# Second layer of a graph network: products with a window of B, from two row groups of the array back into one

## The chip, the cores and the metric

The kernel runs on one core of a Trainium2 chip. Its time is the device time of one execution in microseconds (us); before the change the median of 5 runs is 3966.8 us (3966.45 to 3967.49).

The core has five engines with queues of their own: PE (TensorE, matrix products; its weight loads are listed as PEld), DVE (VectorE, element by element), ACT (ScalarE, activations), POOL (GpSimd, here above all gathers by index) and SP (SyncE, which issues DMA transfers). An engine runs its own instructions in order, and semaphores make one engine wait for another.

## The reference, cut to what matters

There are 12500 nodes with 64 features, and 212500 edges sorted by their target `dst` (12500 of them are loops from a node to itself). Two layers follow each other, each behind a layer norm and a relu:

```python
# layer 1: one 64x64 weight for each of 16 types of edges
msg = sum over r of (h[src] * (etype == r)) @ weight[r]
x = x + segment_sum(msg, dst)

# layer 2: a two-layer network on each edge
hid = relu(concat(h[src], h[dst], edge_attr_8) @ W1 + b1)
x = x + segment_sum(hid @ W2 + b2, dst)
```

W1 has 64 + 64 + 8 rows. So `concat(...) @ W1 + b1` is A[src] + B[dst] + attr @ W1c, with A = h @ W1a + b1 and B = h @ W1b, one row for each node, and W1c the last 8 rows of W1.

## The kernel before, in words

Edges are handled in tiles of P = 128, and G = 4 tiles make a group. Without the loops there are 1563 tiles in 391 groups (the last group has 3). Since edges are sorted by target, the targets of a group lie within a window of W = 40 consecutive nodes, whose first row is read from a table at run time.

The first layer gathers rows of h for each tile and adds them into a table by target and type with one-hot products. As blocks of two times 128 nodes are completed, it makes the rows of A (`a_rows`, for the first four groups `a_early`) and of B (`b_rows`) and stores them. Beside it, in pieces, it sorts the edges' words: `dst_l` gets the place of each edge's target in its group's window, `turned_c` the attributes of the edges (8 rows of 128 edges for a tile), `attr_l` those of the loops.

`second_layer` (line 1449) does the rest, in 391 iterations and some more for the lags. For iteration `it`, with g = it:

- `gather` (line 1005) issues four gathers on POOL, each of 128 rows of A by the tile's sources, into one of 14 buffers of the pool `land` (line 316).
- SP loads the window of B's rows (40 rows of 64) into `b_win[g % 6]`. Below it, `b_win` holds the 8 rows of W1c, loaded once.
- PE makes `pz`, the part of the edges' hidden layer that doesn't come from A: for each tile one product of K = 48 rows. The weights (`of_edges`, 48x128) are the one-hot of the target's place (40 rows) and the edge's attributes (8 rows), and `b_win` moves through.
- Line 1532, three iterations later: DVE adds the gathered rows, `z = pz + a`. Line 1541, four later: ACT makes `hid` = relu(z), and DVE a one-hot `oh` of the place for each edge. Line 1554, six later: PE sums hid over the edges of each target (`pa`). Line 1566, nine later: DVE adds `pa` into `sums`. Towards the end of the run these lags shrink to one or two iterations (`turns`, line 129).
- The one-hot in `of_edges` is made by ACT in two passes, from the places that SP has loaded, the same on all 40 rows (`local_bc`): `off` = |place - row|, then relu(1 - off). The negative row numbers are `neg_w`.

Each product is done in float32, which the trace shows as two MATMUL records, each with its weight load.

Before the change, even and odd tiles of a group use different rows of the array: even tiles have their one-hot, attributes and B rows at partitions 0 to 47, odd tiles at 64 to 111. So B's rows are loaded twice for each group (into both halves), `dst_l` is stored in two rows (even and odd tiles), and `pz` lies in two banks, one for each half. `load_edges` loads places and attributes for a block of RB = 4 groups, a block ahead; `one_hots` makes one half of a block in one call (two passes of 40x1024), in every second iteration, for the block after the present one.

Besides, every eight groups two blocks of 128 nodes become complete: `results` (line 1422) multiplies `sums` with W2, adds x and has ACT issue the store `out<-o`; `own_edges` (line 1400) does the loops of two blocks.

The order is the program's: `V_, S_, T_, Q_, P_` (line 348) issue each instruction behind the one issued last on the same engine, so that DVE, ACT, PE, SP and POOL take the second layer in the order in which the loop body names its instructions. Nearly every one of them is recorded under line 340, the helper that issues them, so the tiles' names tell them apart in the profile.

Of the kernel before, what the change touches and what calls it, by code (L numbers as in the profile page):

```python
# [42 lines left out]
F32 = mybir.dt.float32  # L43
BF16 = mybir.dt.bfloat16
I32 = mybir.dt.int32
AF = mybir.ActivationFunctionType
ALU = mybir.AluOpType
# [5 lines left out]
P = 128  # L53
N = 12500
D = 64
R = 16
EA = 8
# [3 lines left out]
NB = -(-N // P)  # L61
# [12 lines left out]
G = 4  # L74
W = 40
# [9 lines left out]
NGC = -(-NTC // G)  # L85
# [26 lines left out]
KLN = 60  # L112
# [66 lines left out]
WE = W + EA  # L179
EARLY = 4  # L180
NBW = 6
RG = 8
RB = 4
# [26 lines left out]
def gnn_kernel(  # L210
# [13 lines left out]
    attr_c = dram.tile([EC * EA, 1], F32, name="attr_c")  # L224
    attr_l = dram.tile([NB * P * EL, 1], F32, name="attr_l")
    turned_c = dram.tile([NGC * G * EA, P], F32, name="turned_c")
    turned_l = dram.tile([NB * EL, P], F32, name="turned_l")
    src_e = dram.tile([EARLY * 2, 2 * P], I32, name="src_e")
    dst_l = dram.tile([2, NGC * G // 2 * P], BF16, name="dst_l")
    edges_c = dram.tile([EC * 2, 1], I32, name="edges_c")  # L230
# [19 lines left out]

    neg_w = keep.tile([P, 1], F32, name="neg_w")
    for h in range(2):
        G_.iota(neg_w[h * D :][:D], pattern=[[0, 1]], base=0, channel_multiplier=-1, allow_small_or_imprecise_dtypes=True)

# [58 lines left out]
    def in_order():  # L313
        with ExitStack() as c2:
# [98 lines left out]

            b_win = [own.tile([P, D], F32, name=f"b_win{k}") for k in range(NBW)]
            NHID = 6
# [12 lines left out]
            def weights():  # L428
                for k in range(2):
                    Q_.dma_start(wrel[k * D : (k + 1) * D], w_rel[k::2].rearrange("r i o -> i r o"))  # L430
                    Q_.dma_start(w1ab[k * D : (k + 1) * D], w1[: 2 * D].rearrange("(k i) o -> i k o", k=2))
                    yield
                Q_.dma_start(b1_bc, b1.unsqueeze(0).to_broadcast([P, D]))
                Q_.dma_start(t_loop[N:, :].rearrange("n o -> o n"), none)
                Q_.dma_start(attr_l[N * EL :, :].rearrange("(n c) o -> n (c o)", c=EL), zero[: NB * P - N, :EL])
                for t in hid_l:
                    V_.memset(t[:, :, D:], 1.0)
                yield
                Q_.dma_start(w1c, w1[2 * D :])
                Q_.dma_start(place_row, step_2.unsqueeze(0))  # L440
                yield
                Q_.dma_start(w2b[:D, :], w2)
                Q_.dma_start(w2b[D:DA, :], b2.unsqueeze(0))
                yield
                Q_.dma_start(b_rows[NB * P :, :], zero[:W])
                for b in (NB - 2, NB - 1):
                    Q_.dma_start(a_early[b * P : (b + 1) * P, :], zero)
                yield
# [5 lines left out]
            def weights_of_attributes():  # L454
                for t in b_win:
                    for h in range(2):
                        Q_.dma_start(t[h * D + W : h * D + WE, :], w1[2 * D :])
                    yield
# [13 lines left out]
            def places_of(c, psA):  # L472
# [16 lines left out]
                V_.tensor_copy(o[:n], d[:n])  # L489
                for i in range(2):  # L490
                    Q_.dma_start(dst_l[i, b0 // 2 * P : (b0 // 2 + n) * P].rearrange("(r e) -> r e", e=P), o[:n, i, :])
                if c == 0:
# [108 lines left out]
            def loop_attrs(q, psA):  # L601
# [12 lines left out]
                shape, shape2 = [P, m, SUB], [P, m, IN_SUB]  # L614
                V_.tensor_single_scalar(to, firsts, float(NB * P - KLN), op=ALU.min)
                V_.tensor_scalar(to, to, 0.0, float(EL), op0=ALU.max, op1=ALU.mult)
# [832 lines left out]
            def second_layer(ps):  # L1449
# [10 lines left out]
                at, at_b = {}, {}  # L1460
                edges, loaded_edges = {}, {}
                EB = RB * G * P // 2

                def load_edges(b):
                    n = min(EB, NGC * G // 2 * P - b * EB)
                    if n <= 0:
                        return
                    place = wk2.tile([P, EB], BF16, name="local_bc", bufs=2)
                    e = wk2.tile([P, EB], F32, name="of_edges", bufs=3)
                    words = turned_c[b * 2 * EB // P * EA : (b * EB + n) * 2 // P * EA, :].rearrange("(t h c) e -> h c t e", h=2, c=EA)  # L1470
                    for h in range(2):
                        Q_.dma_start(
                            place[h * D : h * D + W, :n], dst_l[h : h + 1, b * EB : b * EB + n].to_broadcast([W, n])
                        )
                        Q_.dma_start(e[h * D + W : h * D + WE, :n].rearrange("c (t e) -> c t e", e=P), words[h])
                    loaded_edges[b] = place, e, n

                def one_hots(b, h):
                    if b not in loaded_edges:
                        return  # L1480
                    place, e, n = loaded_edges[b]
                    rows = slice(h * D, h * D + W)
                    off = wk2.tile([P, EB], BF16, name="off")
                    S_.activation(off[rows, :n], place[rows, :n], AF.Abs, bias=neg_w[rows])
                    S_.activation(e[rows, :n], off[rows, :n], AF.Relu, bias=1.0, scale=-1.0)
                    edges[b] = e

                load_edges(0)
                for h in range(2):
                    one_hots(0, h)  # L1490
                of_z, of_hid, of_pe, of_add = (turns(lag, NGC) for lag in (L2_Z, L2_HID, L2_PE, L2_ADD))
                for it in range(NGC + L2_ADD[1]):

                    g = it
                    if g < NGC:
                        if g % RG == 0:
                            at_b.update(enumerate(windows(first_row, g, PAD_DST, Q_, min(RG, NGC - g)), g))
                        if g % RB == 0:
                            load_edges(g // RB + 1)
                        a_of[g], n_of[g] = gather((a_early if g < EARLY else a_rows)[:, :], src_c, g, NTC)  # L1500
                        n = n_of[g]
                        if n:
                            bw = b_win[g % NBW]
                            now = bass.ds(at_b.pop(g), W)
                            for h in range(2):
                                Q_.dma_start(bw[h * D : h * D + W, :], b_rows[now, :])
                            if g == 1:
# [3 lines left out]
                                for _ in sources_of_last(range(2, EARLY), wk2):  # L1511
                                    pass
                            if g % RB == 0:
                                pz = ps.tile([P, 2, RB, G // 2, D], F32, name="pz", bufs=2)
                            pz_of[g] = pz[:, :, g % RB].rearrange("p h j d -> p j h d")
                            for i in range(n):
                                j, h = divmod(i, 2)
                                at_e = slice((g % RB * G // 2 + j) * P, (g % RB * G // 2 + j + 1) * P)
                                rows = slice(h * D, h * D + WE)
                                more = range(2 if g < EARLY else 0)  # L1520
                                T_.matmul(
                                    pz_of[g][:, j, h, :], lhsT=edges[g // RB][rows, at_e], rhs=bw[rows], start=True, stop=not more
                                )
                                for b in more:
                                    T_.matmul(
                                        pz_of[g][:, j, h, :],
                                        lhsT=of_last[g][b][:, i * P : (i + 1) * P],
                                        rhs=a_last[:, b, :],
                                        start=False,
                                        stop=(b == 1),  # L1530
                                    )
                    for g in of_z.get(it, []):
                        n = n_of[g]
                        if n:
                            hid_of[g] = wk2.tile([P, G, D], F32, name="z", bufs=3)
                            z, a = (t.rearrange("p (j h) d -> p j h d", h=2) for t in (hid_of[g], a_of.pop(g)))
                            pz_g = pz_of.pop(g)
                            for j, h in ((slice(0, n // 2), slice(0, 2)), (slice(n // 2, n // 2 + 1), slice(0, n % 2))):
                                if n % 2 or h.stop == 2:
                                    V_.tensor_tensor(*(t[:, j, h, :] for t in (z, pz_g, a)), op=ALU.add)  # L1540
                    for g in of_hid.get(it, []):
# [12 lines left out]
                    for g in of_pe.get(it, []):  # L1554
                        n = n_of[g]
                        if n:
# [4 lines left out]
                            for i in range(n):  # L1561
                                T_.matmul(pa_of[g], lhsT=r[:, i, :], rhs=o[:, i, :], start=(i == 0), stop=(i == n - 1))
                    if it % 2:
                        one_hots(it // RB + 1, it % RB // 2)
                    next(open_step, None)
# [510 lines left out]
```

## Time and profile before

| | before |
|---|---|
| median of 5 runs | 3966.8 us |
| the profiled execution | 3965.02 us |
| its span, first to last instruction | 3963.1 us |
| first gather of the second layer | 1999.9 us |
| last gather issued | 3952.27 us |
| gathers of the second layer | 1547 of a_rows, 16 of a_early |
| records of pz<-b_win,of_edges on PE | 3126, mean 433 ns |
| loads b_win<-b_rows | 782, 10 KB each |
| loads local_bc<-dst_l | 194 of 80 KB, 2 of 60 KB |
| mean granted clock of TensorE | 0.530 |

The profile comes from one execution, whose span of 3963.1 us lies 1.9 us below its own time. Times of single instructions are from it. Each group of instructions is named by what it writes and reads: `pz<-b_win,of_edges` are the products with the window of B. "Idle before" is the time that the engine had nothing to do just ahead of such instructions, with what ended it. Matmuls are pipelined, so the mean duration of one is longer than the time from one to the next. Gathers overlap in another way: what POOL is busy with is the issuing of a gather, and the rows land later.

### The profile page before, as it was taken

The numbers are of one execution on the slowest core, as the hardware profiler recorded it, in microseconds if no ns is written. First come the engines' busy times: TensorE is split into PE (matmuls) and PEld (weight loads), VectorE is DVE, ScalarE is ACT, GpSimd is POOL, SyncE is SP. The second block draws the span as 40 slices with busy tenths as digits, with TensorE's granted clock in tenths as the row PEclk, the third lists the DMA queues.
The fourth block names the chain that finished last, engine by engine and source line by source line (L and its number), as shares of the span: only waits on it lengthen the run. The fifth ranks groups of instructions, "written<-read, shape, count | busy, mean of one in ns | idle before, by whom it ended". The sixth has DMA issues, their size and how long they took to land. (4 is left out here: it accounts for less than half of the span.)

```text
span 3963.1 us, 53034 instructions
## 1 busy us (share of the span) xinstructions
PE 2186.3 (55%) x14955; PEld 1601.4 (40%) x14955; DVE 1418.8 (36%) x4924; ACT 1647.0 (42%) x3341; POOL 2984.7 (75%) x3170
## 2 busy tenths in 40 slices
PE   1545555555665666666685555555555555555544
PEld 0433333333333333333364444444444444444444
DVE  7895764744743333333321111111111111111112
ACT  6654545544554555554533333323233333333322
POOL 7777777777777777777777777777777777777776
PEclk9655555555555555555555555555555555555555
DMA  5424324225335333333232222222222222222221
GB/s 136 97 46 88 74 46 86 48 46 120 59 49 93 59 59 56 53 57 55 48 66 48 51 48 51 48 51 48 51 48 50 49 48 52 47 52 47 52 47 38
DMA packets 569509, 234.60 MB, mean 59 GB/s; under 512 B 455824, under 2 KB 497680, under 8 KB 568950
## 3 DMA queue, kind: packets, MB, share of 16 engines
q0 software_dynamic: 101152, 111.42, 15.7%
q1 hardware_dynamic: 454757, 116.50, 14.0%
q10 hardware_dynamic: 13298, 3.20, 0.4%
q8 instruction: 123, 2.02, 0.2%
q14 instruction: 179, 1.47, 0.1%
HBM read 195.55 MB, written 35.25 MB: 58 GB/s over the span
## 5 line engine op out<-in xcount | busy, mean ns | idle before, releaser
L340 POOL DMA_INDIRECT rows<-a_rows,src_c x1547 | 1462.1, 945 | 471.6 <-issue 398.5
L340 POOL DMA_INDIRECT rows<-h_rows,src_c x1533 | 1455.0, 949 | 473.3 <-issue 395.9
L340 PE MATMUL pa<-oh_r,rows 128*64 128x96 f32 x6132 | 810.3, 377 | 763.6 <-DMA rows<-h_rows,src_c 614.4
L340 PEld LDWEIGHTS pa<-oh_r,rows 128*64 128x64 f32 x6132 | 470.5, 203 | 1140.3 <-DMA rows<-h_rows,src_c 703.9
L340 DVE TENSOR_TENSOR z<-pz,rows 128x256 f32<-128x256 f32 x392 | 166.0, 423 | 1519.2 <-DMA rows<-a_rows,src_c 1474.5
L340 ACT ACTIVATE hid<-z 128x256 f32<-128x256 f32 x391 | 161.8, 414 | 1075.5 <-DVE z L340 1010.3
L340 DVE TENSOR_TENSOR table<-table,pa 128x96 f32 x1565 | 393.5, 251 | 521.2 <-PE pa L340 439.1
L340 PE MATMUL pa<-oh,hid 128*65 128x40 f32 x3126 | 426.4, 311 | 277.0 <-DVE sums L340 222.7
L340 ACT ACTIVATE off_r<-iota_s,code 128x192 bf16<-128x192 f32 x1535 | 569.7, 444 | 0.0
L340 PE MATMUL pz<-b_win,of_edges 48*128 48x64 f32 x3126 | 504.7, 433 | 79.9 <-ACT of_edges L340 45.0
L340 PEld LDWEIGHTS pa<-oh,hid 128*65 128x65 f32 x3126 | 372.4, 226 | 329.9 <-issue 228.2
L340 PEld LDWEIGHTS pz<-b_win,of_edges 48*128 48x128 f32 x3126 | 412.8, 318 | 144.6 <-ACT of_edges L340 61.8
L340 ACT ACTIVATE oh_r<-off_r 128x768 f32<-128x768 bf16 x392 | 330.2, 842 | 94.5 <-PE pa L340 83.8
L340 ACT ACTIVATE off<-local_bc,neg_w 40x1024 bf16<-40x1024 bf16 x196 | 222.5, 1135 | 5.6 <-DMA local_bc<-dst_l 2.9
L340 ACT ACTIVATE of_edges<-off 40x1024 f32<-40x1024 bf16 x196 | 206.2, 1052 | 6.3
L340 PE MATMUL pT<-table,wrel 128*64 128x256 f32 (+1 forms) x800 | 201.7, 601 | 0.0
L340 DVE SCALAR_TENSOR_TENSOR table<-b_rel,rsel,hT 128x256 f32<-128x256 f32 (+1 forms) x400 | 168.7, 467 | 88.5 <-PE hT L340 67.3
L340 DVE COPY_PREDICATED k_a<-move,k_a 128x1712 int32<-128x1712 int32 (+8 forms) x124 | 186.1, 1501 | 2.1 <-issue 0.2
L340 PE MATMUL po<-ident,hid_l 128*65 128x128 f32 x196 | 54.5, 432 | 200.0 <-ACT hid_l L340 200.0
L340 PE MATMUL po<-w1c,o_at 8*128 8x64 f32 x196 | 53.2, 423 | 170.7 <-DVE sums L340 170.7
L340 PE MATMUL po<-w2b,sums 65*128 65x64 f32 x196 | 53.6, 428 | 156.1 <-DVE sums L340 156.1
L340 ACT COPY table<-table 128x1024 f32<-128x1024 f32 x49 | 51.2, 1044 | 186.3 <-DVE table L340 186.3
(242 smaller groups left out, 1540.7 us busy)
## 6 DMA issues: line engine op xcount, KB each, us to landing
rows<-a_rows,src_c POOLq DMA_INDIRECT x1547
rows<-h_rows,src_c POOLq DMA_INDIRECT x1533
local_bc<-dst_l SPq DMA_DIRECT2D x194, 80.0 KB
b_win<-b_rows SPq DMA_DIRECT2D x782, 10.0 KB
k_a<-in_attr_k SPq DMA_DIRECT2D x72, 144.0 KB
k_a<-in_attr SPq DMA_DIRECT2D x52, 132.0 KB
u_in<-attr_c SPq DMA_DIRECT2D x97, 64.0 KB
turned_c<-u_out SPq DMA_DIRECT2D x97, 64.0 KB
```

The costliest lines, as they stand in the source:

```text
L340: last_ins[self.engine] = getattr(self.engine, name)(*args, **kw)
```

## The change

- The one-hots, attributes and B's rows go back to partitions 0 to 47 for all tiles. `b_win` is 48 rows high, `neg_w` 40.
- B's rows are loaded once for each group, and the attribute weights once for each buffer.
- `dst_l` is stored as one row for each group, in one store where there were two.
- Places and attributes are loaded in one transfer each for a block of four groups, in the block's first iteration, into three buffers each; they were loaded in two transfers each, a block ahead, into two and three buffers.
- The one-hots are made for two groups at a time (again two passes of 40x1024), at the head of every second iteration, just ahead of the products that read them.
- `pz` is a bank for two groups, four buffers of it; z is one addition for the last group too, where it was two.
- `attr_l` gets room for KLN = 60 more nodes, and the clamp of a scatter's first place moves accordingly. This has to do with the first layer only.

The order of the instructions on PE and of the gathers on POOL is the same in both kernels, and so is that on DVE, but for the last group's z. SP has 1959 instructions instead of 2937.

The diff, cut to its core:

```diff
-    dst_l = dram.tile([2, NGC * G // 2 * P], BF16, name="dst_l")
+    dst_l = dram.tile([NGC, G * P], BF16, name="dst_l")
...
-            b_win = [own.tile([P, D], F32, name=f"b_win{k}") for k in range(NBW)]
+            b_win = [own.tile([WE, D], F32, name=f"b_win{k}") for k in range(NBW)]
...
-                Q_.dma_start(attr_l[N * EL :, :].rearrange("(n c) o -> n (c o)", c=EL), zero[: NB * P - N, :EL])
+                Q_.dma_start(attr_l[N * EL :, :].rearrange("(n c) o -> n (c o)", c=EL), zero[: NB * P + KLN - N, :EL])
...
-                    for h in range(2):
-                        Q_.dma_start(t[h * D + W : h * D + WE, :], w1[2 * D :])
+                    Q_.dma_start(t[W:, :], w1[2 * D :])
...
-                for i in range(2):
-                    Q_.dma_start(dst_l[i, b0 // 2 * P : (b0 // 2 + n) * P].rearrange("(r e) -> r e", e=P), o[:n, i, :])
+                Q_.dma_start(dst_l[b0 // G : (b0 + nt) // G, :].rearrange("g (h e) -> (g h) e", h=2), o[:n].rearrange("r i e -> r (i e)"))
...
-                def load_edges(b):
...
-                def one_hots(b, h):
...
-                load_edges(0)
-                for h in range(2):
-                    one_hots(0, h)
...
                         if g % RB == 0:
-                            load_edges(g // RB + 1)
+                            ng = min(RB, NGC - g)
+                            local_bc = wk2.tile([W, RB * G * P], BF16, name="local_bc", bufs=3)
+                            Q_.dma_start(
+                                local_bc[:, : ng * G * P],
+                                dst_l[g : g + ng, :].rearrange("g e -> (g e)").unsqueeze(0).to_broadcast([W, ng * G * P]),
+                            )
+                            of_edges = wk2.tile([WE, RB * G * P], F32, name="of_edges", bufs=3)
+                            Q_.dma_start(
+                                of_edges[W:, : ng * G * P].rearrange("c (t e) -> c t e", e=P),
+                                turned_c[g * G * EA : (g + ng) * G * EA, :].rearrange("(t c) e -> c t e", c=EA),
+                            )
...
-                            now = bass.ds(at_b.pop(g), W)
-                            for h in range(2):
-                                Q_.dma_start(bw[h * D : h * D + W, :], b_rows[now, :])
+                            Q_.dma_start(bw[:W, :], b_rows[bass.ds(at_b.pop(g), W), :])
...
-                            if g % RB == 0:
-                                pz = ps.tile([P, 2, RB, G // 2, D], F32, name="pz", bufs=2)
-                            pz_of[g] = pz[:, :, g % RB].rearrange("p h j d -> p j h d")
+                            if g % 2 == 0:
+                                np_ = min(2, NGC - g)
+                                cols = slice(g % RB * G * P, (g % RB + np_) * G * P)
+                                off = wk2.tile([W, 2 * G * P], BF16, name="off")[:, : np_ * G * P]
+                                S_.activation(off, local_bc[:, cols], AF.Abs, bias=neg_w)
+                                S_.activation(of_edges[:W, cols], off, AF.Relu, bias=1.0, scale=-1.0)
+                                pz = ps.tile([P, 2, G, D], F32, name="pz", bufs=4)
+                            pz_of[g] = pz[:, g % 2]
                             for i in range(n):
-                                j, h = divmod(i, 2)
-                                at_e = slice((g % RB * G // 2 + j) * P, (g % RB * G // 2 + j + 1) * P)
-                                rows = slice(h * D, h * D + WE)
+                                k = (g % RB * G + i) * P
                                 more = range(2 if g < EARLY else 0)
-                                T_.matmul(
-                                    pz_of[g][:, j, h, :], lhsT=edges[g // RB][rows, at_e], rhs=bw[rows], start=True, stop=not more
-                                )
+                                T_.matmul(pz_of[g][:, i, :], lhsT=of_edges[:, k : k + P], rhs=bw, start=True, stop=not more)
...
-                            z, a = (t.rearrange("p (j h) d -> p j h d", h=2) for t in (hid_of[g], a_of.pop(g)))
-                            pz_g = pz_of.pop(g)
-                            for j, h in ((slice(0, n // 2), slice(0, 2)), (slice(n // 2, n // 2 + 1), slice(0, n % 2))):
-                                if n % 2 or h.stop == 2:
-                                    V_.tensor_tensor(*(t[:, j, h, :] for t in (z, pz_g, a)), op=ALU.add)
+                            V_.tensor_tensor(hid_of[g][:, :n, :], pz_of.pop(g)[:, :n, :], a_of.pop(g)[:, :n, :], op=ALU.add)
...
-                    if it % 2:
-                        one_hots(it // RB + 1, it % RB // 2)
```

## The prediction

> **What bounds the kernel now.** I read the busy shares first, then the costliest groups, the waits of POOL, and a stretch of the second layer, where every edited instruction but a few stands.
>
> ```profile
> PE 2186.3 (55%) x14955; PEld 1601.4 (40%) x14955; DVE 1418.8 (36%) x4924; ACT 1647.0 (42%) x3341; POOL 2984.7 (75%) x3170
> ...
> L340 POOL DMA_INDIRECT rows<-a_rows,src_c x1547 | 1462.1, 945 | 471.6 <-issue 398.5
> L340 POOL DMA_INDIRECT rows<-h_rows,src_c x1533 | 1455.0, 949 | 473.3 <-issue 395.9
> ...
> L340 DVE TENSOR_TENSOR z<-pz,rows 128x256 f32<-128x256 f32 x392 | 166.0, 423 | 1519.2 <-DMA rows<-a_rows,src_c 1474.5
> ```
>
> POOL is busy for only 75%, but nearly all of the rest is the gap ahead of each gather: 471.6 us / 1547 = 0.305 us, put down to "issue", a wait for nothing that the profile shows. The waits of POOL say whether a gather is ever held for longer than that (columns: total us, times, longest us):
>
> ```profile
> POOL rows L340 <- issue: 799.0, 2621, 0.3
> POOL rows L340 <- DMA rows<-a_rows,src_c: 71.6, 235, 0.3
> POOL rows L340 <- DMA rows<-h_rows,src_c: 60.1, 197, 0.3
> ...
> POOL rows L340 <- DVE odds L340: 3.5, 1, 3.5
> POOL rows L340 <- DMA attr_c<-k_a,k_to: 3.0, 3, 1.6
> POOL attr_c L340 <- DMA u_in<-attr_c: 2.6, 1, 2.6
> ```
>
> The first three have a longest of 0.3 us, the same gap under other names. So a gather takes 0.945 + 0.30 = 1.25 us whatever the others do, and the real waits of POOL in the whole span are 3.5 + 3.0 + 2.6 us and a 1.1 us one, all in the first layer. The second layer has 1563 gathers (1547 and 16 of a_early): 1563 x 1.249 = 1952 us, from 1999.9 to 3953.2. The group of z above says the same from the other side: 1474.5 of DVE's 1519.2 us of idle time ahead of z are waits for gathered rows, not for the products pz. The page's chain of waits reaches back only 13 us from the end and cannot show this.
>
> Then one stretch of the steady second layer (columns after the stretch: busy us and count of PE, PEld, DVE, ACT, POOL; granted clock, DMA share, GB/s), beside the busiest stretch that DVE has in the first layer:
>
> ```profile
> 200.00:300.00 100.00, 47.76 (x453) 37.12 (x449) 89.81 (x237) 57.34 (x134) 75.73 (x80) 0.60 0.24 49
> ...
> 3000.00:3100.00 100.00, 52.94 (x348) 46.23 (x348) 18.63 (x72) 30.17 (x42) 75.58 (x80) 0.50 0.23 48
> ```
>
> Both hold 80 gathers, with DVE at 90% and at 19%. PE, DVE and ACT have 47, 81 and 70 us of every 100 us left in the second layer. **The kernel ends when the last gather has ended, plus a tail of 10 us.** An edit counts only if it touches POOL's gathers, holds one of them up, or lies in that tail.
>
> **The change, part by part.**
>
> *POOL.* Its order of gathers is unchanged; one of two iotas for neg_w goes (0.32 us for two, so 0.16 us) ahead of the first gather at 3.3 us. At 50.6 us POOL waits 3.5 us for DVE (odds, the row above), which hides it: 0. If that cover were gone: -0.2 us.
>
> *PE, the products with B.* The count stays: 4 matmuls a group, two records each, in the same order among the others. What goes is that they alternate between rows 0 to 47 and 64 to 111 of the array. The time of it is in the timeline of PE (start, us, operation, records):
>
> ```profile
> 2019.18 1.11 PE L340 MATMUL pz<-a_last,raw_rows 128*128 128x64 f32 x4
> 2020.23 0.69 PE L340 MATMUL pz<-b_win,of_edges 48*128 48x64 f32 x2
> ...
> 3006.84 1.12 PE L340 MATMUL pz<-b_win,of_edges 48*128 48x64 f32 x8
> 3007.89 1.10 PE L340 MATMUL pa<-oh,hid 128*65 128x40 f32 x8
> ```
>
> From start to next start, 8 records in two row groups take 1.05 us, and 4 records of the same shape that use all rows also take 1.05 us (2019.18 to 2020.23). po<-w1c, with 8 rows only, takes 1.04 us for 4 (2025.21 to 2026.25), so it isn't the number of rows. I take 2.10 us for a group in place of 1.05: +1.05 us. Between 2100 and 3900 us are 1441 gathers, 360 groups, and PE is busy for 959 us; 959 + 360 x 1.05 = 1337 us, 74% of 1800. Cover: 1.29 us of idle PE a group stay. Cost 0. From the other side, if the records overlapped as now, 0 too; if each waited out its own 433 ns (mean of the group), it is the first rival.
>
> The Trainium skill, "TensorE: Matmul & The Clock Gate", decision table, speaks against this change: products over few rows, laid on separate row groups, run concurrently, and one alone takes as long as one over 128 rows. By that rule, on a path that PE sets, 391 x 1.05 = 411 us would come on top; the rows above agree on the factor of 2, but they put it on an engine that waits.
>
> *ACT, the one-hots.* 196 pairs of 40x1024 before; 391 groups by two make 196 pairs after, the same elements: 1135 + 1052 ns each, 0 difference in busy time. They move: before they are made a block of four groups ahead, after in the iteration that needs them, ahead of hid of group g-4. This adds a wait: off of group g waits on ACT for the load of the same block. Behind it on ACT stand hid, hid_l and the store of the output, and pa on PE and the sums on DVE wait for hid. A pz(g) is needed only when the gathers of g have landed. In PE's order it follows pa(g-7), whose rows landed some 7 x 5.0 = 35 us earlier, so 2.2 us of ACT and 2.1 of PE fit. And POOL doesn't notice a late z at once: 14 buffers of gathered rows (line 316) hold 14 x 5.0 = 70 us of gathers. Cost 0; the price without that cover is the second rival.
>
> *SP.* For four groups it issues 8 loads of B's rows and 4 of places and attributes; after, 4 and 2, with places and attributes in the same bytes. B's rows fall from 782 x 10 KB to 391 x 10 KB, 3.9 MB of some 96 MB that move in the second layer (49 GB/s), so about 1 of the 24 points of DMA share. What less traffic is worth to a gather: 949 ns at a share of 0.35 (mean of the stretches from 100 to 2000 us) against 945 at 0.24 is 0.36 ns a point; 1547 x 0.36 = -0.6 us. Bounds: 0, and all gathers at the shortest one seen (940 ns): 1547 x -5 = -7.7 us. I take -0.6, from the nearest rows.
>
> *First layer.* One store of places in place of two (8 pairs), 6 loads of the attribute weights fewer, a fill of 104 rows in place of 44. All are SP's, while POOL waits for DVE or its own scatters. Bounds: all of the real waits above go or are doubled, -/+8.4 us (each less its 0.3 us gap). I take 0.
>
> *Tail.* The last group has three tiles. Before, z is two additions and only the second, 128x64, follows the last landing; after, one of 128x192:
>
> ```profile
> 3952.27 2.86 DMA rows<-a_rows,src_c
> ...
> 3955.16 0.24 DVE z L340
> ```
>
> 128x128 takes 283 ns (o<-po) and 128x256 takes 423, so 0.35 in place of 0.24: +0.1 us. Products of the last group are ready well before: now at 3949.1 us, after 1.3 us of ACT and 1.6 of PE that start when hid of group 388 is done (3946.9), so about 3949.8, against 3955.1.
>
> **Sum**: 0 + 0 + 0 - 0.6 + 0 + 0.1 = -0.5 us. The profiled execution took 3965.0 us (span 3963.1 and 1.9 around it), the median is 3966.8; the -0.5 us makes 3964.5 there and 3966.3 on the median. A measurement of this kernel can tell about 0.2%, 7.9 us, from no change.
>
> **Rivals.**
> 1. *PE becomes the bound (slower).* Place: pz in the second layer. For: one row group halves the rate, and PE rises from 53 to 74%. Against: the two rows of 1.05 us. It decides from (1800 - 959) / 360 = 2.34 us more a group, 3.39 us for 8 records, 424 ns each. At 433 ns, one by one: 3.46 us, 2.41 more, 959 + 869 = 1828 us for 1800, and over 391 groups +30 us: **3997**. With each weight load (318 ns) unhidden as well: 8 x 0.751 = 6.0 us, 959 + 360 x 4.96 = 2745 for 1800, over 391 groups +1026 us: **4993**. 3 in 100.
> 2. *ACT stands at each block for its load (slower).* For: SP idles for 21.6 us at the longest for the store of the output, and the load isn't ahead any more. Against: a load issued at 2014.66 let ACT go on at 2017.02, 2.4 us later; ACT's work for a block is 4 x 0.41 + 2 x 2.19 = 6.0 of 20 us, so it decides from 14 us a block. At 21.6 + 2.4 = 24 us in every second block (an output each 8 groups): 49 x 10 = +490 us: **4457**. 2 in 100.
> 3. *Gathers quicken (faster).* If traffic set their length, all would go to 940 ns: 3966.8 - 7.7 = **3959**; more would take the 0.30 us gap. The skill's page "SBUF — State Buffer" warns that DVE can lock GpSimd out of writing descriptors; the stretches with 90% and 19% of DVE busy, 80 gathers each, show no such loss to win back. Beyond 0.2%: 3 in 100.
> 4. *The change doesn't do what it says*: PE's time for pz stays at 1.05 us, or the granted clock, 0.50 here and 1.00 in the first 100 us, rises and takes it back. The end is the same, 3966.3; it lies within the forecast.
>
> **Numbers.** Forecast, POOL sets the end: 92 in 100, 3966.3. The range takes in the -7.7 of the gathers and the +8.4 of the first layer's waits: 3959 to 3975. Faster 0.03, within 0.2% 0.92, slower 0.05.
>
> **What would show it.** After: 80 gathers in each 100 us, mean 945; POOL's waits over 0.3 us still only in the first layer; pz about 2.1 us a group from start to start, PE near 74% of the second layer; z still waiting for gathered rows; SP with half of its b_win loads. It is wrong if rows<-a_rows waits for z, pz or a buffer for more than 0.3 us, or if z waits for of_edges, pz or local_bc for hundreds of us.

## The result, and the profile after

The changed kernel takes 3966.63 us (median of 24 runs) against 3966.78 us (44 runs of the kernel before): a ratio of 1.0000, 95% interval 0.9995 to 1.0006. It is no change that can be measured.

| | before | after |
|---|---|---|
| the profiled execution | 3965.0 us | 3969.3 us |
| its span | 3963.1 us | 3967.4 us |
| first group of the second layer gathered (its last gather issued) | 2003.6 us | 2007.1 us |
| group 388 gathered | 3943.4 us | 3947.5 us |
| between the two | 1939.8 us | 1940.4 us |

The profiled execution of the changed kernel is 4.3 us longer, but 3.5 us of that are there before the second layer has gathered its first group; the stretch that the change is about differs by 0.6 us. Over all runs nothing is left of it.

The page after, the lines that answer to those shown of before:

```profile
PE 2452.2 (62%) x14955; PEld 1878.3 (47%) x14955; DVE 1419.4 (36%) x4923; ACT 1641.7 (41%) x3341; POOL 2989.3 (75%) x3169
...
L339 POOL DMA_INDIRECT rows<-a_rows,src_c x1547 | 1462.7, 946 | 471.5 <-issue 406.0
...
L339 PE MATMUL pz<-b_win,of_edges 48*128 48x64 f32 x3126 | 771.5, 424 | 351.2 <-ACT of_edges L339 346.1
...
L339 DVE TENSOR_TENSOR z<-pz,rows 128x256 f32<-128x256 f32 x391 | 165.9, 424 | 1487.6 <-DMA rows<-a_rows,src_c 1401.5
```

The line of pz before the change, which the prediction didn't show:

```profile
L340 PE MATMUL pz<-b_win,of_edges 48*128 48x64 f32 x3126 | 504.7, 433 | 79.9 <-ACT of_edges L340 45.0
```

PE is busy for 266 us more, all of it in pz (504.7 us before, 771.5 after), and PE now stands idle ahead of pz for 346 us, waiting for the one-hots (45.0 before). Both are large, and neither shows in the end. POOL's line is what it was: 946 ns a gather, 471.5 us of gaps. The waits of POOL (total us, times, longest):

```profile
POOL rows L339 <- issue: 807.7, 2650, 0.3
POOL rows L339 <- DMA rows<-a_rows,src_c: 63.4, 208, 0.3
...
POOL rows L339 <- DMA attr_c<-k_a,k_to: 3.7, 4, 1.2
POOL rows L339 <- DVE odds L339: 3.5, 1, 3.5
POOL attr_c L339 <- issue: 3.4, 4, 2.5
```

From 2000 us to the end no wait of POOL is longer than 0.3 us, so again only the first layer has longer ones, much the same as before. The steady second layer from 2100 to 3900 us, before and after, and the stretch shown before (busy us and count of PE, PEld, DVE, ACT, POOL; granted clock, DMA share, GB/s):

```profile
2100.00:3900.00 1800.00, 959.18 (x6288) 835.55 (x6288) 337.29 (x1311) 542.93 (x763) 1360.80 (x1441) 0.50 0.24 49
...
2100.00:3900.00 1800.00, 1216.67 (x6334) 1102.46 (x6333) 336.35 (x1311) 536.64 (x761) 1361.17 (x1440) 0.50 0.23 47
3000.00:3100.00 100.00, 67.84 (x356) 61.55 (x355) 18.74 (x74) 29.89 (x42) 75.62 (x81) 0.50 0.22 45
```

PE has gone from 53 to 68% with POOL where it was. The products of one group, in the timeline of PE:

```profile
3001.61 1.97 PE L339 MATMUL pz<-b_win,of_edges 48*128 48x64 f32 x8
3003.50 0.95 PEld L339 LDWEIGHTS pa<-oh,hid 128*65 128x65 f32 x8
3003.51 1.10 PE L339 MATMUL pa<-oh,hid 128*65 128x40 f32 x8
```

From start to next start the 8 records of pz take 1.90 us in place of 1.05: two row groups had been worth a factor of 1.8.

### The profile page after: what moved, and what is told of

It reads as the page before. It is cut to its first block, busy times and chain, and to the rows that moved or that the text cites. A ratio compares the mean times of both kernels' runs of the same rounds, so it can differ in the third digit from the quotient of the medians.

```text
span 3967.4 us, 51512 instructions
## 1 busy us (share of the span) xinstructions
PE 2452.2 (62%) x14955; PEld 1878.3 (47%) x14955; DVE 1419.4 (36%) x4923; ACT 1641.7 (41%) x3341; POOL 2989.3 (75%) x3169
## 5 line engine op out<-in xcount | busy, mean ns | idle before, releaser
L339 POOL DMA_INDIRECT rows<-a_rows,src_c x1547 | 1462.7, 946 | 471.5 <-issue 406.0
L339 PE MATMUL pz<-b_win,of_edges 48*128 48x64 f32 x3126 | 771.5, 424 | 351.2 <-ACT of_edges L339 346.1
L339 PEld LDWEIGHTS pz<-b_win,of_edges 48*128 48x128 f32 x3126 | 696.0, 325 | 412.1 <-ACT of_edges L339 388.0
L339 ACT ACTIVATE off<-local_bc,neg_w 40x1024 bf16<-40x1024 bf16 x196 | 222.2, 1134 | 17.3 <-DVE sums L339 16.1
L339 ACT ACTIVATE hid_l<-o_ab 128x128 f32<-128x128 f32 x49 | 15.2, 311 | 259.4 <-DVE o_ab L339 259.4
L339 DVE TENSOR_TENSOR oh<-local,iota_p 128x160 f32<-128x160 f32 x391 | 120.9, 310 | 0.0
```

The source lines that it names most:

```text
L339: last_ins[self.engine] = getattr(self.engine, name)(*args, **kw)
```

## The experiments

The theory: POOL's gathers, 1.25 us each, set the end, and everything that the change does lies on engines that wait for them. The rivals: PE's new load or new waits are on the path, but something else made up for them; or the traffic that fell was worth something. All kernels below are small edits of the two. pz_plus2 and loads5 ran ten times each, the others once. The measure for all of them is the kernel before on the same chip: its median of 13 runs was 3969.9 us beside the first four and 3970.0 beside the last three.

### More work for PE: two and four products more a group

```diff
+    for _ in range(1 if i < 2 and g >= EARLY else 0):    # pz_plus4: i < 4
+        T_.matmul(pz_of[g][:, i, :], lhsT=of_edges[:, k : k + P], rhs=bw, start=True, stop=True)
     T_.matmul(pz_of[g][:, i, :], lhsT=of_edges[:, k : k + P], rhs=bw, start=True, stop=not more)
```

Two products more (pz_plus2):

> The changed kernel with two of the four products of a group with B issued twice (from the fifth group on; the repeat writes the same result again, so nothing is left out). This adds 4 MATMUL records a group, 4 x 0.236 = 0.95 us of PE by the changed kernel's 1.89 us for 8. Theory (POOL's gathers set the end, 1.25 us each, and PE has room): PE goes from 68% to about 86% of the second layer and the time stays at 3966.6 within 4 us. Rival (PE's waits for the one-hots, 340 us in 360 groups of the changed kernel, are a fixed part of its loop): 3.38 + 0.95 + 0.95 = 5.27 us a group against 5.00 of POOL, 391 x 0.27 = +106 us, about 4073.

Measured: 3971.2 us beside 3969.9 of the kernel before, a ratio of 1.0004 (0.9994 to 1.0014). The steady second layer:

```profile
2100.00:3900.00 1800.00, 1522.13 (x7821) 1414.62 (x7822) 338.83 (x1322) 540.87 (x768) 1361.45 (x1440) 0.50 0.24 48
```

PE is busy for 85% and POOL still makes its 1440 gathers. In this stretch PE's waits for the one-hots fell from 340 to 237 us: they are slack, and are used up as work is added. The rival's 4073 us is out.

Four products more (pz_plus4):

> The same with all four products of a group issued twice: 8 records more a group, +1.89 us of PE, 3.38 + 1.89 = 5.27 us a group against POOL's 5.00. Theory: this is past the point at which PE takes over, so the second layer takes 391 x 5.27 = 2061 us in place of 1952, about 4076, POOL waits for buffers, and z waits for pz. Rival (the waits for the one-hots stay in PE's loop): 6.22 us a group, 2432 us, about 4446. If the time stays at 3967, PE has room that the busy time does not show and the theory falls.

Measured: 4009.5 us, 40 us over the kernel before, where the theory had expected 110.

```profile
2100.00:3900.00 1800.00, 1793.20 (x9188) 1705.00 (x9188) 331.75 (x1304) 516.58 (x760) 1361.15 (x1441) 0.50 0.24 47
```

PE has no idle time left, and POOL still isn't held up: 1441 gathers. How both can be is shown by the lag of each group's z (its start, less the start of the group's last gather), read off the timelines of DVE and POOL:

| group | before | after | pz_plus4 |
|---|---|---|---|
| 0 | 43.5 us | 27.8 us | 27.9 us |
| 10 | 12.1 | 17.6 | 29.6 |
| 20 | 2.5 | 2.6 | 28.9 |
| 200 | 3.2 | 2.6 | 27.2 |
| 340 | 2.6 | 2.7 | 25.2 |
| 388 | 2.6 | 2.6 | 47.9 |

At the start of the second layer each kernel is 28 to 44 us behind with z. The changed kernel catches up within 20 groups, as the one before does. With four products more PE just keeps POOL's pace: the lag stays at 25 to 30 us over 340 groups, so PE needs 5.0 us a group, not the 5.27 expected. The 16 records of a group take 3.60 us there, from start to next start:

```profile
2701.20 3.67 PE L339 MATMUL pz<-b_win,of_edges 48*128 48x64 f32 x16
...
2704.80 1.10 PE L339 MATMUL pa<-oh,hid 128*65 128x40 f32 x8
```

The lag rises only within the last 40 groups, in which the lags of the loop shrink to one or two iterations and PE waits for the group it has just prepared. The last z of all starts 46.6 us behind its gather, where the changed kernel has 3.0: these are the 40 us, about half of them the lag that stood there all along. Nothing there holds POOL up, since the 14 buffers are worth 70 us. So the point from which PE decides is where it was looked for, within 6%, and the changed kernel, at 68%, is well below it.

### Less work for POOL: half of the gathers left out

```diff
-    for i in tiles:
+    for i in tiles[:only]:                               # only=2 in the second layer
         P_.indirect_dma_start(out=t[:, i, :], ...)
...
+    a = a_of.pop(g)[:, :2, :].unsqueeze(1).to_broadcast([P, 2, 2, D])
```

In the changed kernel (half_after):

> The changed kernel with only the first two of the four gathers of each group of the second layer; the two others are left out, and the rows of the first two are added to the products of all four tiles, so the output is not the reference's. POOL then needs 2.50 us a group. Theory: PE is the bound with 3.38 us a group, 391 x 3.38 = 1322 us in place of 1952, about 3337. Rival (waits for the one-hots stay, 0.95 us a group): 4.33 us, 1693 us, about 3708. If the second layer stays near 1952 us, it was not the gathers that set the end.

In the kernel before (half_before):

> The kernel before the change, with the same two gathers of each group left out. PE's busy time is 2.66 us a group (959 us for 360) and POOL's 2.50. Theory: 391 x 2.66 = 1040 us in place of 1952, about 3055, and not below 2992 (POOL's 977 us); so the change would cost about 280 us here, where PE is on the path. Rival (the change costs nothing even on PE's path, or both kernels meet another bound first): both halves within 30 us of each other.

Measured: 3351.4 us (3337 expected) and 3028.2 us (3055 expected). The second layer follows the gathers down, and now the two kernels differ by 323 us. The same stretch of both; first half_after, the changed kernel:

```profile
2100.00:2950.00 850.00, 850.00 (x4540) 786.42 (x4539) 232.98 (x938) 373.49 (x548) 488.84 (x519) 0.50 0.24 52
```

and half_before, in the same columns:

```profile
2100.00:2950.00 850.00, 847.09 (x6091) 761.72 (x6090) 315.85 (x1264) 513.04 (x735) 642.82 (x680) 0.50 0.34 73
```

In the changed kernel PE is busy without a gap and POOL makes 519 gathers; before the change, in the same 850 us, 680 at the full pace of 1.25 us. The records of pz in this stretch, half_after first (busy us and count of PE, PEld, DVE; granted clock, DMA share, GB/s):

```profile
2100.00:2950.00 850.00, 509.53 (x2074) 460.75 (x2073) 107.46 (x259) 0.50 0.24 52
...
2100.00:2950.00 850.00, 387.98 (x2768) 322.97 (x2768) 145.60 (x348) 0.50 0.34 73
```

At eight records a group, a group takes 3.28 and 2.46 us; (3.28 - 2.46) x 391 = 321 us. That this comes so near to 323 is partly luck, for half_before is close to two bounds at once: its z is 45.7 us behind the gathers at group 0, 14.7 at group 200 and 2.6 at group 350, so by then PE has caught up with POOL. Read from z to z, the two kernels differ by 310 us between groups 0 and 350 and by 31 us from there to the end, and the first z of half_before comes 17 us later, which takes 17 off. And in the changed kernel POOL now has what it never had in the full one, waits for its buffers (POOL, total us, times, longest):

```profile
POOL rows L339 <- DVE oh L339: 225.0, 94, 3.8
POOL rows L339 <- issue: 119.6, 391, 0.6
```

So where PE sets the pace two row groups are worth some 0.82 us a group, and the full kernel doesn't see it because the gathers hide it.

### Less work for PE: half of the products left out (pz_half)

```diff
+    if g >= EARLY and i >= 2:
+        continue
     T_.matmul(pz_of[g][:, i, :], lhsT=of_edges[:, k : k + P], rhs=bw, start=True, stop=not more)
...
+    pz_g = pz_of.pop(g)[:, :2, :].unsqueeze(1).to_broadcast([P, 2, 2, D]) if g >= EARLY else ...
```

> The changed kernel with the products with B of two of the four tiles of a group left out (from the fifth group on; the products of the first two tiles are added to all four, so the output is not the reference's). This gives PE back about 0.95 us a group, what the change took from it. Theory: PE falls from 68% to about 49% of the second layer, and the time doesn't move, within 4 us of the kernel before. Rival (what the change costs PE is on the path, and something else made up for it): 391 x 0.8 to 0.95 = 310 to 370 us faster.

Measured: 3966.0 us in one run, 4 us below the median of the kernel before, whose own runs go from 3967.3 to 3971.5. PE is busy for 901.8 of 1800 us, 50%, and POOL makes its 1441 gathers. The rival's 310 us or more are not there: what the change costs PE is not on the path.

### More traffic: B's rows loaded five times (loads5)

```diff
-    Q_.dma_start(bw[:W, :], b_rows[bass.ds(at_b.pop(g), W), :])
+    at_g = at_b.pop(g)
+    Q_.dma_start(bw[:W, :], b_rows[bass.ds(at_g, W), :])
+    for _ in range(4):
+        Q_.dma_start(wk2.tile([W, D], F32, name="b_more", bufs=16), b_rows[bass.ds(at_g, W), :])
```

> The changed kernel with each window of B's rows loaded five times: the further four go to a tile that nobody reads, so nothing is left out. This adds 391 x 4 x 10 KB = 15.6 MB, four times what the change took away, on the same queue. Theory (a gather's length is POOL's own): by the -0.6 us that the prediction gave to a fall of one point of DMA share, four points more are +2.2 us, so no measurable difference from the kernel before, gathers of a_rows at 945 to 947 ns. Rival (traffic sets the gather's length; the change won time there and lost it elsewhere): well above 947 ns, and over 8 us slower.

Measured: 3967.5 us beside 3970.0 of the kernel before, a ratio of 0.9995 (0.9985 to 1.0005). The gathers:

```profile
L339 POOL DMA_INDIRECT rows<-a_rows,src_c x1547 | 1460.7, 944 | 471.7 <-issue 406.2
```

The DMA share went from 0.23 to 0.27 and the gather from 946 to 944 ns. Traffic of this size doesn't set a gather's length, and taking 3.9 MB away left it at 946 ns for 945.

### The one-hots late, with two row groups (half_late)

```diff
-    load_edges(0)
-    for h in range(2):
-        one_hots(0, h)
...
-    load_edges(g // RB + 1)
+    load_edges(g // RB)
+    for h in range(2):
+        one_hots(g // RB, h)
...
-    if it % 2:
-        one_hots(it // RB + 1, it % RB // 2)
```

Half of the gathers are left out as above.

> The kernel before the change with half of the gathers left out as in half_before (two row groups, 3028 us there), but with places, attributes and one-hots made late: a block of four groups is loaded and its four passes of ACT run at the head of the block, just ahead of the products that read them. This takes the part of the change that moves the one-hots, and more of it (4.4 us of ACT at once), without the part that goes to one row group. Theory (the 323 us between half_after and half_before are all PE's rate): PE still has its one-hots in time, 3028 within 15 us. Rival (the one-hots made late cost PE a wait where it is the bound): at least 2.2 us for each of 98 blocks, +215 us, about 3243 or more.

Measured: 3077.2 us, 49 us above half_before. It is neither: the theory's 15 us were too few and the rival's 215 far too many. In the steady part about one group in eight (some 40 of 334 between 2100 and 2950 us) is held for a moment by the second half of the four passes, and its eight records take 1.90 us, from 2705.08 to 2706.98 here, in place of 1.05:

```profile
2705.08 0.69 PE L340 MATMUL pz<-b_win,of_edges 48*128 48x64 f32 x2
...
2705.94 1.11 PE L340 MATMUL pz<-b_win,of_edges 48*128 48x64 f32 x6 [0.18 <-issue]
...
2706.98 1.10 PE L340 MATMUL pa<-oh,hid 128*65 128x40 f32 x8
```

This is 0.85 us in eight groups, 0.11 us a group; between z of group 0 and z of group 350 the kernel loses 37 us on half_before in this way. From there to the end it loses 15 more (its first z had come 3 us earlier), where the lags shrink and PE stands between the halves:

```profile
2990.70 0.68 PE L340 MATMUL pz<-b_win,of_edges 48*128 48x64 f32 x2 [2.15 <-ACT of_edges L340]
...
2992.95 0.92 PEld L340 LDWEIGHTS pz<-b_win,of_edges 48*128 48x128 f32 x6 [1.76 <-ACT of_edges L340]
```

So lateness has a price where PE is the bound, though with four passes at once. The change makes two at a time, and in half_after pz waits for of_edges for 12.3 us in all. Between 2100 and 2950 us no group is held there: each takes 1.89 or 1.90 us from the first record of pz to the next product. So lateness is little of the 323 us, and the rate of PE is the rest. A kernel with one row group and the one-hots a block ahead was not run.

## Why the prediction was right, point by point

The mechanism held: POOL's gathers set the end, and what the change costs lies on engines that wait for them. That the forecast of 3966.3 us lies 0.3 us from the median is luck, since runs of one kernel spread over some 4 us and the -0.6 us in the sum has no support.

- *What bounds the kernel.* Right, and shown from both sides: PE's load in the second layer went from 50 to 85% (pz_half, after, pz_plus2) with the time within 0.2%, and halving the gathers took 619 us off the changed kernel and 942 off the one before (from 3969.9).
- *POOL, and its iota.* Right: the wait for odds is 3.5 us as before, and hides the iota.
- *PE.* The mechanism was right, the size too large: +1.05 us a group by the rows of a_last and po, where 1.90 - 1.05 = +0.85 was measured, and PE at 68% where 74 was said. Neighbouring rows of other shapes gave the factor of 2 where 1.8 was measured, 10% off. On a path that PE sets, 0.82 to 0.85 us a group make 321 to 332 us of the 411 worked out; half_after and half_before differ by 323.
- *ACT.* The cost was right (0), but the wait that was named didn't come: between 2100 and 3900 us no wait of ACT is for a load of places (`off` waits for 16.1 us in all, 0.6 at the longest). Another came, which the prediction didn't name: pz stands behind of_edges for 340 us of that stretch (44 before), and z for 62 us behind pz (before, for 14 us behind of_edges). The timeline shows why. On ACT the one-hots stand behind hid, hid waits for z, and z for the gathered rows:

```profile
3014.61 0.42 DVE L339 TENSOR_TENSOR z<-pz,rows 128x256 f32<-128x256 f32 x1 [4.11 <-DMA rows<-a_rows,src_c]
...
3015.13 0.42 ACT L339 ACTIVATE hid<-z 128x256 f32<-128x256 f32 x1 [4.45 <-DVE z L339]
...
3015.45 1.13 ACT L339 ACTIVATE off<-local_bc,neg_w 40x1024 bf16<-40x1024 bf16 x1
...
3016.62 1.06 ACT L339 ACTIVATE of_edges<-off 40x1024 f32<-40x1024 bf16 x1
...
3017.73 1.96 PE L339 MATMUL pz<-b_win,of_edges 48*128 48x64 f32 x8 [3.89 <-ACT of_edges L339]
```

  So this wait of PE follows from the gathers and doesn't hold them up. The prediction said that z would go on waiting for gathered rows, and so it did for 1372 us of that stretch. The slack in PE's order covered the rest, as pz_plus2 shows, in which these waits shrink.
- *SP, fewer loads.* The -0.6 us has no support: the gather is at 946 ns with less traffic and at 944 with five times the loads, so no run shows this term. The difference of 4 ns between the layers, from which it was made, has another cause, which stays open.
- *First layer.* 0 within what runs differ by. The longer span of the profiled execution comes mostly from there (3.5 of 4.3 us), and disappears in the median.
- *Tail.* The last z went from 0.24 to 0.37 us, +0.13 for +0.1, read in the chain of waits after; the last group's products end at 3954.4 us, 4.9 us ahead of its rows, where 5.3 was worked out:

```profile
3956.35 2.86 DMA rows<-a_rows,src_c
...
3959.33 0.37 DVE z L339
```

- *The rivals.* PE as the bound was to decide from 3.39 us of pz a group. In pz_plus4 pz takes 3.6 us (16 records from 2701.20 to 2704.80), and PE runs level with POOL: the point lies near 3.6. It was put too low because the busy share of a waiting engine was taken for its need: 959 us for 360 groups are 2.66 us, but in half_before, back to back, a group takes 2.46. The second rival's wait of ACT for its load didn't come at all; a smaller loss from lateness shows only where PE is the bound. Rival 3 fell, since the gathers stayed at 946 ns, and with loads5, since traffic doesn't set their length. Of rival 4, neither happened: pz did slow down, and the granted clock of the second layer stayed at 0.50.

## What to carry to other kernels

Find the engine whose instructions follow each other with a constant gap from end to end, even if the profile calls it 75% busy: here the gap of 0.30 us ahead of each gather was part of its price, and the other engines' idle time was its shadow. What the gap is made of stays open. A change to a waiting engine, even one that nearly halves the rate of its main product, was worth nothing here, and would be until that engine reached the pace of the bound; so measure its worth in a copy in which the bound is lightened, as half of the gathers did here (323 us), before keeping or dropping it. An engine's busy time while it waits overstates what it needs back to back (2.66 against 2.46 us here).

## What the runs showed of the hardware that was not expected

- TensorE's granted clock stayed at 0.50 in half_after while PE was busy for all of 850 us, and was 1.00 in the first 100 us, with PE busy for 11%. The Trainium skill, "TensorE: Matmul & The Clock Gate", part 1 (the HAM clock gate), has the gate open to the full rate after some 3.4 us of sustained work; these products did not open it, and why stays open.
- Gathers took 1.25 us each whether DVE was busy for 90% or 19% of the time, PE for 50 or 100%, and the DMA share 0.23 or 0.34.
- Two row groups gave a factor of 1.8 (8 records of 48 rows in 1.05 us against 1.90), with both halves in one instruction stream.
